# Pairing the projections and re-accounting the filler work in a fused attention and convolution kernel

## The chip, the core and the metric

The kernel runs on one core of a Trainium2 chip, in float32. The metric is device time in microseconds (us), the median of several executions. TensorE does the matrix products, VectorE (DVE) and ScalarE (ACT) the elementwise work, SyncE (SP) issues the loads and stores. GpSimd does almost nothing here. [...]

## The reference

Four layers run one after the other on 16 images of 384 channels and 16 x 16 pixels, seen as 2 clips of 8 frames.

```python
# layer 0: attention over the 2048 pixels of a clip, 12 heads of 32 channels, no value projection
qk = (xt @ qk_w.T).reshape(B, N, 2, nh, HEAD_DIM)
attn = softmax(einsum('bhnd,bhmd->bhnm', q * scale, k), axis=-1)
attn = alpha * eye + beta * attn - gamma * Cm          # Cm is 1/N everywhere
out = einsum('bhnm,bhmd->bhnd', attn, v)               # v is the input itself
# layer 1: 7x7 depthwise convolution, layer norm, 384 -> 1536 -> 384 with gelu and a response norm, residual
# layer 2: Sobel edges, 768 -> 384, layer norm, gelu, residual
# layer 3: 1x1, 3x3 depthwise, 1x1, linear attention, projection, layer norm, MLP 384 -> 1536 -> 384
```

## The kernel before, in words

The pixels of a clip are 4 blocks of 512 (`BLK`). A *unit* of attention is one clip and one group of 128 channels (4 heads); there are 6 units, so 24 blocks of queries. For each block the kernel goes through 16 key tiles of 128. One such round is a *step*, so attention has 384 steps.

In a step `scores` (line 435) makes the scores of four heads in two tiles `st` of two PSUM banks each (from `bank2`, line 385, a pool of three tiles), and ScalarE writes their exponentials to two tiles `e`. `weighted` (line 453) works one step behind: four products of exponentials and values into `av`, then VectorE's adds, which sum the exponentials over groups of four steps in the tiles `s` (steps 1, 2 and 3 of each group have a pair of adds). The sums go through TensorE into the denominators `dn` in four quarter-wide pieces, one per step, the first two steps after the group's last add; the last group of a block goes in one wide piece. `due` is a table from step number to such later work. `finish` (line 508) reads `dn` to `r` on ScalarE; four reciprocals, the scaling of `va` and the write to `l` follow on VectorE, one per step. In `scale` (line 519) ScalarE also passes over `r` to a tile `junk` for the sum that a safety check needs.

Queries and keys of a unit are projected by `qk` (line 397): three products of 128 channels into one bank, then a copy, on ScalarE for a query and on VectorE for a key. The first block of keys and queries and the other keys are needed when a unit starts, the other queries during it. They are called at the steps that `SLOTS` names: steps 0, 4 and 8 of a unit's first block, 0 and 4 of the second and third, 0 of the fourth.

`fill` (line 1444) is called at the end of each step with the projection's time in `added`. It places other work between: the taps of layer 1's 7 x 7 convolution (`convolutions`, line 829; one ScalarE operation and 48 VectorE operations `y<-l` per channel group), and every fourth step one operation of `lead`, layer 1's first block. A single running credit, `room`, says how many taps may be placed. When attention is over, a planner (`Plan.all`, line 180) orders all the remaining work by estimated start times, with the ranks in `RANK` and the tolerance `SLACK`. TensorE, ScalarE and VectorE then run exactly the order in which the program issued the work.

After attention the names are: `ph_l` and `po_l` for layer 1's two wide products, `su` and `sv` for the sums behind a layer norm, `pf` for layer 2, `l3a`, `l3b`, `l3c` for layer 3, whose last part is the MLP with `ph_l3c` and `po_l3c`.

Of the kernel before, what the change touches and what calls it, by code (L numbers as in the profile page):

```python
# [11 lines left out]
ALU = mybir.AluOpType  # L12
# [5 lines left out]
NC = C // P  # L18
# [10 lines left out]
NBLK = N // BLK  # L29
NIP = NBLK  # L30
NQC = N // P
SLOTS = ((0, 4, 8), (0, 4), (0, 4), (0,))
FIRST = NQC + 10

TURNS = (
# [6 lines left out]
    (0, ((1, 1), (1, 2), (1, 3),)),  # L42
    (1, ((0, 3), (1, 0), (1, 3), (1, 2), (1, 1),)),
)
AFTER = ('hid', 0, 2, 1)

RANK = {
    "mid": ((-4.2, 20.2, -65.9, 40.3), (11.6, 63.7, 50.6, 36.1)),
    "l1": ((-28.5, 90.6, 6.7, 64.2), (55.1, 56.5, 16.9, 27.6)),
    "l3c": ((32.8, 24.4, 106.0, 83.3), (3.4, 80.2, 74.5, 60.5)),  # L50
    "conv": 93.3,
}
SLACK = 0.142
JUNK = 2
ADDS = ((4, 4, 4, 4), (4, 4, 4, 4))
XB, YB, SB = 12, 2, 22
TB = BLK // P
RB = 2 * HW
# [132 lines left out]
            self.step(min((s for s in starts if s[0] <= first), key=lambda s: (s[1], s[0]))[2])  # L191


class Task:


    def __init__(self, name, rank, ops):
        self.name, self.rank, self.ops = name, rank, ops
        self.head = next(ops, None)

    def advance(self):
        self.head = next(self.ops, None)


def channel_means(dve, pool, X, cols, b):
# [162 lines left out]
def attention(tc, X, xt, L0, block, small, col, cols, ones, load_qk, banks, fill, bound):  # L368
# [6 lines left out]
    with ExitStack() as actx:  # L375
# [9 lines left out]
        def bank2(name):  # L385
            return pst.tile([P, 2, BLK], F32, tag="st", name=name)
# [4 lines left out]
        def projections(b, g):  # L391


            made = {w: [None] * NBLK for w in "qkv"}
            u = b * NC + g

            def qk(j, n):
                w = "qk"[j]
                pp = bank2(f"p{w}_{u}_{n}")
                for c in range(NC):  # L400
                    pe.matmul(
                        pp[:, 0, :],
                        wqk_sb[:, g, j, c, :],
                        X[b][n][:, c, :],
                        start=(c == 0),
                        stop=(c == NC - 1),
                    )
                o = made[w][n] = small(f"{w}_{u}_{n}")
                (act.copy if j == 0 else dve.tensor_copy)(o, pp[:, 0, :])
                return 2.7 - 0.6 * j  # L410

            def values(n):
                o = made["v"][n] = small(f"v_{u}_{n}")
                nc.sync.dma_start(o, xt[b, g, n])

            def key(n):
                values(n)
                return qk(1, n)

            step = lambda f, *a: lambda: f(*a)  # L420
            early = [step(key, 0), step(qk, 0, 0)] + [step(key, n) for n in range(1, NBLK)]
            late = [step(qk, 0, n) for n in range(1, NBLK)]
            return made, early, late

# [3 lines left out]
        def unit(u, made, gm):  # L428

            b, g = units[u]  # L430
            q, keys, v = made["q"], made["k"], made["v"]
            adds = ADDS[b]
            acc, sums = {}, {}

            def scores(n, t):
# [17 lines left out]
            def weighted(n, t, es):  # L453
                if t == 0:
                    acc["av"] = pacc.tile([P, BLK], F32, tag="av", name=f"av_{u}_{n}")
                for h in range(4):
                    pe.matmul(
                        acc["av"][HD * h : HD * (h + 1), :],
                        v[t // TB][:, (t % TB) * P + HD * h : (t % TB) * P + HD * (h + 1)],
                        es[h // 2][:, h % 2, :],  # L460
                        start=(t == 0),
                        stop=(t == NQC - 1),
                    )
                at = t % adds[n]
# [12 lines left out]
                if at == adds[n] - 1:  # L477
                    parts = 1 if t == NQC - 1 else adds[n]
                    for i in range(parts):
                        due.setdefault(k + 2 + i, []).append(  # L480
                            lambda i=i, summed=dict(sums): weights(
                                n, t, summed, ts(i, BLK // parts)
                            )
                        )
# [23 lines left out]
            def finish(n, va, xg):  # L508

                if g == 0:  # L510
                    L0[b][n] = block(f"l0_{b}_{n}")
                k = u * NBLK + n
                r = op.tile([P, BLK], F32, tag="r", name=f"r_{u}_{n}")
                act.activation(r, acc["dn"], AF.Identity, accum_out=bound[:, 0, k : k + 1])

                def invert(i):
                    dve.reciprocal(r[:, ts(i, P)], r[:, ts(i, P)])

                def scale():
                    junk = op.tile([P, BLK], F32, tag="junk", name=f"junk_{u}_{n}", bufs=1)  # L520
                    act.activation(junk, r, AF.Identity, accum_out=bound[:, 1, k : k + 1])
                    dve.tensor_tensor(va, va, r, ALU.mult)

                def put():
                    dve.scalar_tensor_tensor(
                        L0[b][n][:, g, :], va, col("beta", g), xg, ALU.mult, ALU.add
                    )

                todo = [*(lambda i=i: invert(i) for i in range(TB)), scale, put]
                for i, f in enumerate(todo):  # L530
                    due.setdefault((k + 1) * NQC + 2 + i, []).append(f)

            return scores, weighted
# [2 lines left out]
        for b, (_, steps) in enumerate(means):  # L536
            for i, s in enumerate(steps):
                due[b * NC * NBLK * NQC - 36 * b + 3 * i] = [s]
        made, early, late_steps = projections(*units[0])
        for s in early:  # L540
            s()
        before = None
        for u, (b, g) in enumerate(units):
            steps = late_steps
            scores, weighted = unit(u, made, means[b][0][:, g : g + 1])
            if u + 1 < len(units):
                made, early, late_steps = projections(*units[u + 1])
                steps = steps + early
            for n in range(NBLK):
                for t in range(NQC):  # L550
                    es = scores(n, t)
                    added = 0.0
                    if before:
                        before()
                    before = lambda f=weighted, a=(n, t, es): f(*a)
                    if t in SLOTS[n]:
                        added = steps.pop(0)() if steps else 0.0
                    fill((u * NBLK + n) * NQC + t, added)
            assert not steps
        before()  # L560
# [7 lines left out]
def conv_seq_kernel(  # L568
# [869 lines left out]
    if fast:  # L1438
        open_pool("s", SB)
        open_pool("tiny", 2)  # L1440

        room = 0.0

        def fill(t, added=0.0):
            nonlocal room
            if t < 0:
                while plan.step(bias):
                    pass
                return


            if t % NQC == 9 and t > NQC:
                u, i = divmod(t // NQC - 1, NBLK)
                plan.mark(("l0", u // NC, i, u % NC))
            room = min(3.0, room + 2.25 + added - 2.28 * (t % 4 != 1) - 0.8 * (2 < t % NQC < 9))
            if NC * NBLK * NQC - 36 < t <= NC * NBLK * NQC - 21 and t % 3 == 0:
                room -= 1.7
            if ("y", 0, 0, NC - 1) in plan.made and t % 4 == 1 and plan.holds(lead, "wa"):
                room -= lead.head.length if lead.head.engine == "DVE" else 0.0
                plan.step(lead)  # L1460
            while t >= FIRST and room > 0 and ("y", 0, YB - 1, NC - 1) not in plan.made:
                if not plan.step(conv):
                    break
                room -= 0.57

        attention(
            tc, X, xt, L0, block, small, col, cols, ones, first_loads, banks, fill, bound
# [132 lines left out]
```

## Time and profile before

| | us |
|---|---|
| median of three executions | 2695.55 |
| lowest and highest | 2694.98, 2695.66 |
| the profiled execution: its time | 2696.76 |
| its span, first to last instruction | 2695.0 |
| attention, first score to first hidden product of layer 1 | 22.6 to 1061.4 |
| busy: ScalarE, whole span | 1560.4 |
| adds of exponentials on VectorE (384 and 192) | 444.8 and 225.6 |
| taps of the 7 x 7 convolution on VectorE (1152) | 658.9 |

The profile gives one execution. Busy time of TensorE comes from modelled ends of pipelined products, so that a product which waits for the next can look busy. Each product of float32 appears as two records. In the lists, `out<-in` names the tiles, the number after the bar is the sum of busy time and the mean of one, and the last part is the idle time of the engine just before and what ended it. All arithmetic instructions carry the line of one helper (L96), so tiles are the names to go by.

### The profile page before, as it was taken

The numbers are of one execution on the slowest core, as the hardware profiler recorded it, in microseconds if no ns is written. First come the engines' busy times: TensorE is split into PE (matmuls) and PEld (weight loads), VectorE is DVE, ScalarE is ACT, GpSimd is POOL, SyncE is SP. The second block draws the span as 40 slices with busy tenths as digits, with TensorE's granted clock in tenths as the row PEclk, the third lists the DMA queues.
The fourth block names the chain that finished last, engine by engine and source line by source line (L and its number), as shares of the span: only waits on it lengthen the run. The fifth ranks groups of instructions, "written<-read, shape, count | busy, mean of one in ns | idle before, by whom it ended". The sixth has DMA issues, their size and how long they took to land. (4 is left out here: it accounts for less than half of the span.)

```text
span 2695.0 us, 33760 instructions
## 1 busy us (share of the span) xinstructions
PE 2656.3 (99%) x13477; PEld 1069.1 (40%) x13477; DVE 1996.9 (74%) x2586; ACT 1560.4 (58%) x2282; POOL 7.4 (0%) x54
## 2 busy tenths in 40 slices
PE   9999999999999999999999999999999999999999
PEld 3333333333332323445444444444454444454443
DVE  5899999999999989799999669999904535313120
ACT  5787787778877787565645372533665633125221
POOL 0000000000000000000000000000000000000000
PEclk9999999999999999999999999999999999999999
DMA  3000000000000002100111112121000110000000
GB/s 149 1 17 1 5 13 1 13 5 2 16 1 1 13 1 95 35 0 1 36 36 36 39 46 68 59 71 47 16 8 0 35 36 0 12 1 13 12 4 21
DMA packets 34421, 65.17 MB, mean 24 GB/s; under 512 B 1872, under 2 KB 17360, under 8 KB 34256
## 3 DMA queue, kind: packets, MB, share of 16 engines
q1 hardware_dynamic: 34112, 62.79, 7.1%
q8 instruction: 107, 1.75, 0.3%
q14 instruction: 58, 0.48, 0.1%
q10 hardware_dynamic: 144, 0.15, 0.0%
HBM read 56.64 MB, written 6.29 MB: 23 GB/s over the span
## 5 line engine op out<-in xcount | busy, mean ns | idle before, releaser
L96 ACT ACTIVATE e<-st 128x1024 f32<-128x1024 f32 x768 | 743.5, 1022 | 175.5 <-PE st L96 169.7
L96 DVE SCALAR_TENSOR_TENSOR y<-l,vec,y 128x420 f32<-128x420 f32 (+8 forms) x1152 | 658.9, 632 | 18.8 <-ACT y L96 13.4
L96 PE MATMUL st<-q,k 32*128 32x512 f32 x3072 | 464.5, 643 | 8.6 <-DVE k L96 3.3
L96 DVE TENSOR_TENSOR s<-s,e 128x1024 f32<-128x1024 f32 x384 | 444.8, 1209 | 2.8 <-ACT e L96 2.8
L96 PE MATMUL av<-e,v 128*32 128x512 f32 x3072 | 411.9, 607 | 0.7 <-ACT va L96 0.7
L96 PE MATMUL po_l<-hid_l,wb 128*128 128x512 f32 x576 | 258.2, 602 | 7.3 <-ACT hid_l L96 7.2
L96 PE MATMUL ph_l<-y,wa 128*128 128x512 f32 x576 | 258.6, 594 | 1.0 <-ACT y L96 1.0
L96 PE MATMUL ph_l3c<-d_l3c,wa 128*128 128x512 f32 x576 | 257.2, 593 | 0.0
L96 PE MATMUL po_l3c<-hid_l3c,wb 128*128 128x512 f32 x576 | 254.1, 593 | 0.0
L96 DVE TENSOR_TENSOR s<-e,e 128x1024 f32<-128x1024 f32 x192 | 225.6, 1216 | 33.0 <-PE dn L96 19.3
L96 ACT ACTIVATE hid_l3c<-ph_l3c,vec 128x512 f32<-128x512 f32 x96 | 65.8, 686 | 248.0 <-PE ph_l3c L96 247.8
L96 PEld LDWEIGHTS st<-q,k 32*128 32x128 f32 x3072 | 137.1, 183 | 170.3 <-issue 99.9
L96 PEld LDWEIGHTS av<-e,v 128*32 128x32 f32 x3072 | 60.6, 108 | 294.0 <-issue 286.1
L96 PEld LDWEIGHTS po_l<-hid_l,wb 128*128 128x128 f32 x576 | 110.4, 193 | 145.9 <-issue 131.5
L96 PEld LDWEIGHTS ph_l3c<-d_l3c,wa 128*128 128x128 f32 x576 | 108.9, 190 | 136.5 <-issue 129.8
L96 PEld LDWEIGHTS ph_l<-y,wa 128*128 128x128 f32 x576 | 108.3, 190 | 137.2 <-issue 126.2
L96 PEld LDWEIGHTS po_l3c<-hid_l3c,wb 128*128 128x128 f32 x576 | 108.7, 190 | 133.2 <-issue 129.6
L96 PEld LDWEIGHTS dn<-s,ones 128*32 128x32 f32 x2496 | 81.8, 111 | 187.4 <-issue 174.5
L96 DVE SCALAR_TENSOR_TENSOR o_l3c<-po_l3c,vec,l 128x512 f32<-128x512 f32 x24 | 17.6, 742 | 170.7 <-PE po_l3c L96 170.0
L96 PE MATMUL dn<-s,ones 128*32 128x128 f32 (+1 forms) x2496 | 142.4, 299 | 0.0
L96 ACT ACT_TABLE_LOAD x103 | 132.1, 1283 | 7.5 <-PE ph_l L96 5.4
L96 ACT ACTIVATE hid_l<-ph_l,vec 128x512 f32<-128x512 f32 x96 | 65.6, 683 | 119.4 <-PE ph_l L96 118.8
(155 smaller groups left out, 2480.5 us busy)
## 6 DMA issues: line engine op xcount, KB each, us to landing
wa<-in_w_dram SPq DMA_DIRECT2D x12, 768.0 KB, 4.5
wb<-in_w_dram SPq DMA_DIRECT2D x12, 768.0 KB, 4.6
wa<-in_mlp_w_dram SPq DMA_DIRECT2D x12, 768.0 KB, 4.5
wb<-in_mlp_w_dram SPq DMA_DIRECT2D x12, 768.0 KB, 4.5
x<-in_x_dram SPq DMA_DIRECT2D x8, 768.0 KB, 10.7
v<-in_xt_dram SPq DMA_DIRECT2D x24, 256.0 KB, 2.7
out_dram<-o_l3c SPq DMA_DIRECT2D x24, 256.0 KB, 2.0
qkv<-in_qkv_wT_dram SPq DMA_DIRECT2D x3, 576.0 KB, 11.1
```

What stands on the lines that cost most here:

```text
L96: self.last = self.tc.keep_in_program_order(make(*args, **kw))
```

## The change

The projections are made in pairs: one tile of two banks takes two of them, and there is one pair per block of queries, at step 5. The keys and queries of the opening are paired too. The credit of `fill` is replaced by an account: `pace` gives for each step the time of TensorE and of VectorE, what VectorE is behind is carried to the next step as `lag`, and taps are placed while at least 0.4 us is free. A tap that must wait for the one before costs 0.12 more in the account. The first operation of a chunk, on ScalarE, ends a step's placing. The pass over `r` for the check stands in a function of its own and is due four steps later. `ADDS` has another form with the same values. The ranks, the tolerance and the point after which the second clip's convolution may begin (`AFTER`) have other values.

```diff
-SLOTS = ((0, 4, 8), (0, 4), (0, 4), (0,))
+SLOT = 5
-AFTER = ('hid', 0, 2, 1)
+AFTER = ('x4', 0, 1)
 RANK = {
...
-SLACK = 0.142
+SLACK = 0.122
...
+def pace(t):
+    n, i = divmod(t - 1, NQC)
+    adds = ADDS[n]
+    stride = adds // 4
+    pe, dve = 2.066, 2.275 if t and i % adds else 0.0
+    at = i - adds - 1
+    if at >= 0 and at % adds % stride == 0 and at % adds < 4 * stride and i > adds:
+        pe += 0.22
+    elif i == 1 and n > 0:
+        pe += 0.87
+    else:
+        pe += 0.09
+    if n > 0:
+        dve += {2: 0.88, 3: 0.88, 4: 0.88, 5: 0.88, 6: 0.6, 7: 0.66}.get(i, 0.0)
+    return pe, dve
...
-            def qk(j, n):
+            def qk(j, n, pp):
                 w = "qk"[j]
-                pp = bank2(f"p{w}_{u}_{n}")
                 for c in range(NC):
                     pe.matmul(
-                        pp[:, 0, :],
+                        pp,
...
-                (act.copy if j == 0 else dve.tensor_copy)(o, pp[:, 0, :])
+                (act.copy if j == 0 else dve.tensor_copy)(o, pp)
                 return 2.7 - 0.6 * j
...
                 def scale():
+                    dve.tensor_tensor(va, va, r, ALU.mult)
+
+                def check():
                     junk = op.tile([P, BLK], F32, tag="junk", name=f"junk_{u}_{n}", bufs=1)
                     act.activation(junk, r, AF.Identity, accum_out=bound[:, 1, k : k + 1])
-                    dve.tensor_tensor(va, va, r, ALU.mult)
...
-                for i, f in enumerate(todo):
+                for i, f in [*enumerate(todo), (8, check)]:
                     due.setdefault((k + 1) * NQC + 2 + i, []).append(f)
...
+        def project(name, steps):
+            pp = bank2(name)
+            return sum(f(pp[:, i, :]) for i, f in enumerate(steps))
+
         made, early, late_steps = projections(*units[0])
-        for s in early:
-            s()
+        for i in range(0, len(early), 2):
+            project(f"p_{i}", early[i : i + 2])
...
-                    if t in SLOTS[n]:
-                        added = steps.pop(0)() if steps else 0.0
+                    if t == SLOT and steps:
+                        added = project(f"p_{u}_{n}", steps[:2])
+                        del steps[:2]
                     fill((u * NBLK + n) * NQC + t, added)
...
-            room = min(3.0, room + 2.25 + added - 2.28 * (t % 4 != 1) - 0.8 * (2 < t % NQC < 9))
-            if NC * NBLK * NQC - 36 < t <= NC * NBLK * NQC - 21 and t % 3 == 0:
-                room -= 1.7
+            length, work = pace(t)
+            free = length + added - work - lag
+            if NC * NBLK * NQC - 36 < t <= NC * NBLK * NQC - 21 and t % 3 == 1:
+                free -= 1.7
             if ("y", 0, 0, NC - 1) in plan.made and t % 4 == 1 and plan.holds(lead, "wa"):
-                room -= lead.head.length if lead.head.engine == "DVE" else 0.0
-                plan.step(lead)
-            while t >= FIRST and room > 0 and ("y", 0, YB - 1, NC - 1) not in plan.made:
+                if plan.step(lead) and lead.at.engine == "DVE":
+                    free -= lead.at.length
+            ops = []
+            while t >= FIRST and ("y", 0, YB - 1, NC - 1) not in plan.made:
+                op = conv.head
+                if op.engine == "DVE":
+                    if free < 0.4:
+                        break
+                    free -= op.length + 0.12 * (op.after[0] in ops[-1:])
                 if not plan.step(conv):
                     break
-                room -= 0.57
+                ops.append(op)
+                if op.engine == "ACT" and conv.head.engine == "DVE":
+                    break
+            lag = max(0.0, -free)
```

More of the change, by code (lines that the diff above doesn't have):

```diff
@@ L44 @@
 )
-AFTER = ('hid', 0, 2, 1)
+AFTER = ('x4', 0, 1)
 RANK = {
[L48 to L51, printed above, removed]
+    "mid": ((-16.9, 20.2, -65.9, 50.2), (11.6, 60.8, 50.6, 36.1)),
+    "l1": ((-41.0, 15.6, 6.7, 54.8), (53.9, 56.5, 16.9, 46.3)),
+    "l3c": ((37.9, 24.4, 106.0, 83.2), (3.4, 41.2, 70.0, 60.5)),
+    "conv": 97.9,
 }
-SLACK = 0.142
+SLACK = 0.122
 JUNK = 2
-ADDS = ((4, 4, 4, 4), (4, 4, 4, 4))
+ADDS = (4,) * 24
 XB, YB, SB = 12, 2, 22
@@ L191, in all @@
             self.step(min((s for s in starts if s[0] <= first), key=lambda s: (s[1], s[0]))[2])
+def pace(t):
[13 more added lines that the diff above has]
+    return pe, dve
 class Task:
     def __init__(self, name, rank, ops):
-        self.name, self.rank, self.ops = name, rank, ops
+        self.name, self.rank, self.ops, self.at = name, rank, ops, None
         self.head = next(ops, None)
     def advance(self):
-        self.head = next(self.ops, None)
+        self.at, self.head = self.head, next(self.ops, None)
 def channel_means(dve, pool, X, cols, b):
@@ L414, in values, with key @@
                 nc.sync.dma_start(o, xt[b, g, n])
-            def key(n):
+            def key(n, pp):
                 values(n)
-                return qk(1, n)
-            step = lambda f, *a: lambda: f(*a)
+                return qk(1, n, pp)
+            step = lambda f, *a: lambda pp: f(*a, pp)
             early = [step(key, 0), step(qk, 0, 0)] + [step(key, n) for n in range(1, NBLK)]
@@ L431, in unit @@
             q, keys, v = made["q"], made["k"], made["v"]
-            adds = ADDS[b]
+            adds = ADDS[u * NBLK : (u + 1) * NBLK]
             acc, sums = {}, {}
@@ L477, in weighted @@
                 if at == adds[n] - 1:
-                    parts = 1 if t == NQC - 1 else adds[n]
+                    parts = 1 if t == NQC - 1 else 4
                     for i in range(parts):
-                        due.setdefault(k + 2 + i, []).append(
+                        due.setdefault(k + 2 + i * adds[n] // 4, []).append(
                             lambda i=i, summed=dict(sums): weights(
@@ L1440, in conv_seq_kernel @@
         open_pool("tiny", 2)
-        room = 0.0
+        lag = 0.0
         def fill(t, added=0.0):
-            nonlocal room
+            nonlocal lag
             if t < 0:
```

## The prediction

> **What bounds the kernel now.** I read the page first, then the windows by stage, then the groups by line, then the timeline. The page's row of TensorE and the windows of attention, handover, and the two later stretches:
>
> ```profile
> PE 2656.3 (99%) x13477; PEld 1069.1 (40%) x13477; DVE 1996.9 (74%) x2586; ACT 1560.4 (58%) x2282; POOL 7.4 (0%) x54
> ...
> 28.00:1061.40 1033.40, 1024.16 (x8881) 323.61 (x8873) 960.46 (x1031) 819.85 (x943) 0.00 (x0) 1.00 0.02 6
> 1061.40:1125.00 63.60, 54.88 (x135) 24.55 (x134) 47.15 (x73) 47.60 (x109) 0.00 (x0) 0.92 0.38 135
> 1125.00:1620.00 495.00, 486.99 (x1425) 223.79 (x1424) 437.70 (x674) 269.05 (x482) 2.55 (x18) 0.99 0.09 28
> 1620.00:2690.00 1070.00, 1068.59 (x2988) 488.19 (x2986) 545.56 (x787) 417.33 (x740) 4.19 (x30) 1.00 0.08 24
> ```
>
> The columns are TensorE, weight loads, VectorE, ScalarE, GpSimd, granted clock, DMA share, GB/s. TensorE is the bound everywhere, and from 1125 us on it is nearly seamless (about 9 us idle in 1565). So the change can win only in attention and the handover. In attention VectorE is busy 960 of 1033 us, so a second engine runs close behind.
>
> "99%" hides stalls, because a modelled matmul can stretch. I took the distance from each step's first score matmul to the next. A bare step is 2.066 us, one with the quarter sums (dn) 2.286, the one with the wide dn 2.94, and a projection adds 2.77. The floor of attention is then 384 x 2.066 + 24 x (12 x 0.22 + 0.87) + 43 x 2.77 = 996.6 us. Observed, from the first score at 22.6 to the first hidden matmul at 1061.4, it is 1038.8. So 42 us are stall. Where they come from is seen in one block:
>
> ```profile
> 436.90 1.14 PE L96 MATMUL st<-q,k 32*128 32x512 f32 x8
> 437.97 1.06 PE L96 MATMUL av<-e,v 128*32 128x512 f32 x8
> 438.03 0.95 DVE L96 RECIPROCAL r<-r 128x128 f32<-128x128 f32 x1
> 438.85 0.40 PE L96 MATMUL dn<-s,ones 128*32 128x128 f32 x8
> 438.89 2.29 DVE L96 TENSOR_TENSOR s<-s,e 128x1024 f32<-128x1024 f32 x2
> 439.01 0.63 ACT L96 ACTIVATE junk<-r 128x512 f32<-128x512 f32 x1 [1.28 <-DVE r L96]
> 439.18 1.13 PE L96 MATMUL st<-q,k 32*128 32x512 f32 x4
> 439.55 0.19 ACT L96 ACTIVATION_READ_ACCUMULATOR junk<-r 128x1 f32 x1
> 439.64 3.75 ACT L96 ACTIVATE e<-st 128x1024 f32<-128x1024 f32 x4
> 440.70 1.13 PE L96 MATMUL st<-q,k 32*128 32x512 f32 x4 [0.39 <-ACT e L96]
> ```
>
> The check sum (junk) stands in ScalarE's queue ahead of the next exponentials and waits for VectorE's last reciprocal. The exponentials come late, the score banks stay full, and the second half of the scores starts 1.5 us after the first. Steps 9 of all blocks hold 13 of the 42 us; most of the rest lies in steps 4 to 8.
>
> The copies out of a projection, which the change moves:
>
> ```profile
> L96 DVE COPY k<-pk 128x512 f32<-128x512 f32 x24 | 16.2, 676 | 34.0 <-PE pk L96 34.0
> L96 ACT COPY q<-pq 128x512 f32<-128x512 f32 x24 | 14.1, 586 | 47.0 <-PE pq L96 47.0
> ```
>
> Both engines already stand still for TensorE there. In the timeline a copy starts 0.11 us after the next score matmul (pq from 602.93, scores 605.70, q 605.81).
>
> [...] The halves of a pair are two banks[...]; no run here shows whether one is placed. In the built order of the changed kernel one is: the first matmul of each second half lists a wait on ScalarE (on VectorE where the first half is a key). The slot's earlier reader is a ScalarE exponential, so at the key pairs nothing but the first half's copy explains VectorE. [...] the trace agrees with six windows (or runs) of 3.41 us at half clock after stalls, the one around 1116 us three windows long.
>
> **The change, part by part.** The built lists hold the same instructions before and after. Only order differs; after 1.15 ms only some VectorE neighbours swap and, at the very end, hidden matmuls of the last block alternate with output matmuls of the one before. TensorE is seamless there and the inputs (d_l3c) are ready at 2590 for 2596: nothing gained or lost.
>
> *Check sum later.* It now stands at step 11, when the reciprocals are long done. What remains of the 42 us: the score-exponential loop at step 4 (0.17 x 24 = 4), layer 1's two early sums (2 us of matmul and about 4 of table loads on ScalarE), the drain at the end (3). So 29 of 42 go: **-29** (22 to 33).
>
> *Pairs.* Two halves of six passes at 0.427 us are 2.56 each, plus 0.21 for changing tile form. Between them TensorE waits: the last pass ends, the copy starts (0.11 after the point where scores would start), lasts 0.59, and is seen about 0.05 later; against an unbroken stream that is 1.0, with the slower first pass 1.1 us. A pair takes 2.56 + 1.1 + 2.56 + 0.21 = 6.43 against 2 x 2.77 = 5.54: 0.89 x 21 = **+18.7** (10 to 26; below 0.7 the copy alone forbids). Behind the wait stand scores, hence everything. In the five key-key pairs VectorE must first work off its queue: summing its rows from one dn to the next it arrives about 0.9 late, **+4** (0 to 8). The three opening pairs have two such waits: **+2**.
>
> *Taps by the account.* In 13 of the blocks a key is the last half of the pair, so VectorE's copy stands until the projection ends, 2 to 5 us idle, and the 4 to 8 taps that the account grants for the projection's time stand behind the copy. From the start of the next step S: copy 0.11 + 0.61, taps n x 0.66 (start to start within one chunk; 0.55 where two chunks alternate), then adds of steps 5 to 7, a reciprocal and va: 8.3 us from the first to the last end in the block above (435.76 to 444.06). The sums are ready at S + 9.0 + taps. TensorE wants them at S + 4 x 2.286 + 2.05 = S + 11.2, 11.1 with the signal. So 2.1 us of taps are free. The list has 6, 5, 6, 6, 5, 6, 5, 8, 6, 7, 7, 6 taps there, and 4 plus two channel means (1.66 each) in the thirteenth: stalls of 1.7, 1.2, 1.45, 1.9, 1.2, 1.45, 1.2, 2.3, 1.2, 1.9, 1.8, 1.2 and 3.7, together **+22** (6 to 30). In before such sums ended up to 1.1 after the step began, about 1 us inside the limit, so it was not binding. Blocks whose pair is two queries escape.
>
> *Handover.* 266 taps stand before the last add, against 279; layer 1's first block starts later (its sum moved by 24 steps), so its last scaling falls behind the final check sum:
>
> ```profile
> 1061.39 10.57 PE L96 MATMUL ph_l<-y,wa 128*128 128x512 f32 x24
> 1074.18 1.12 PE L96 MATMUL su_l<-s_l,ones 128*128 128x512 f32 x2 [2.22 <-DVE s_l L96]
> ...
> 1065.71 0.63 ACT L96 ACTIVATE junk<-r 128x512 f32<-128x512 f32 x1 [3.52 <-DVE r L96]
> ```
>
> From the end T of attention, the first hidden column stops at its third chunk until junk (T + 4.9) and a scaling of 0.8 are done: 4 us. VectorE then does 4.9 of finish, 18 taps (10.4), weight means (5.8), the weight scaling (1.5), 4 taps and two adds (3.6): su at T + 27, TensorE there at T + 24. Then sv at T + 34, the next block's scaled input at T + 46, po at T + 53.1, where it was 1108.9, T + 47.5: **+5.6** (2 to 9). TensorE's weights arrive earlier (ca lands near T + 18), so no DMA decides.
>
> *Sum.* -29 + 18.7 + 4 + 2 + 22 + 5.6 = +23 on the profiled span of 2695.0, whose execution took 2696.8; the median of the three is 2695.55. Carried to the median: 2719. Attention would end near 1079.
>
> **Rivals.** *The pair wait alone* (chance 0.17): the sums come in time, since VectorE had 73 us idle in attention and the late-sum figure rests on a chain of six durations. For it: dn waited for s only 8 us before. Against: the taps stand behind the copy. 2719 - 22 = 2697.
> *Faster* (0.10), one mechanism: the second half of a pair doesn't really wait, its place being the listed wait on ScalarE. If this were the old exponential, long over, the pair saves 0.21 x 21 = 4.4, TensorE gives VectorE time for the taps and the sums come within the limit; -29 - 4.4 + 5.6 gives 2668. It decides once a first copy lands before its second half's first pass. Against: VectorE is named at the key pairs.
> *Half clock* (0.15): 34 new stalls of 1 to 4 us, and each window of 3.41 us at half costs 1.7. Before, stalls of 2 to 5 us were followed by one, one of 2.2 at 1072 was not. Ten more give +17: 2736.
>
> **How the numbers follow.** The forecast (0.58) is 2719, by itself 2706 to 2732. About 0.2% (5.4 us) is what a measurement of this kernel tells from no change. The pair wait alone splits into 0.03 faster, 0.09 same, 0.05 slower; so faster 0.13, same 0.09, slower 0.78. A range of 2692 to 2738 leaves out the faster case and the ends, about 0.18.
>
> **What would show it.** Right: some 21 idle times of about 1 us of TensorE before p, ended by copies of q (16) or k (5); dn waiting for s by some 20 us in all; junk's idle time (9 us before) near nothing; ph_l stopped some 4 us by y. Wrong: pairs of 5.3 us, attention ending before 1050, or new losses after 1150 us, which would mean that the later order matters more than its few swaps suggest.

## The result and the profile after

The changed kernel takes 2737.65 us (median of 4 runs, 2735.56 to 2737.73) against 2695.27 for the kernel before (4 runs): ratio 1.0156, interval 1.0138 to 1.0174. It is slower by 42 us where 23 were forecast. The profiled execution has a span of 2735.8 us where before had 2695.0.

First the page's rows of TensorE and VectorE, then the same four stages as windows (columns as before: TensorE, weight loads, VectorE, ScalarE, GpSimd, granted clock, DMA share, GB/s). Attention now ends at 1095.3 us.

```profile
PE 2665.1 (97%) x13477; PEld 1070.3 (39%) x13477; DVE 1997.9 (73%) x2586; ACT 1557.4 (57%) x2282; POOL 7.4 (0%) x54
...
30.00:1095.30 1065.30, 1031.11 (x8875) 325.13 (x8871) 951.51 (x1018) 814.98 (x941) 0.00 (x0) 1.00 0.02 6
1095.30:1166.00 70.70, 56.81 (x138) 25.18 (x137) 55.50 (x86) 48.90 (x110) 0.00 (x0) 0.95 0.34 121
1166.00:1661.00 495.00, 486.98 (x1422) 223.79 (x1421) 439.27 (x678) 268.86 (x482) 2.55 (x18) 0.99 0.09 28
1661.00:2730.00 1069.00, 1068.42 (x2987) 488.11 (x2986) 544.01 (x785) 417.29 (x740) 4.19 (x30) 1.00 0.07 24
```

TensorE is 97% busy instead of 99, and the missing time lies in the first two windows: in attention it idles for 34 us of 1065 instead of 9. The last two stages are as they were. The end of attention moved by 33.9 us (1061.4 to 1095.3), and what follows it takes 6.9 us more (1633.6 to 1640.5).

The groups of instructions that the prediction named, in the changed kernel:

```profile
L97 PE MATMUL dn<-s,ones 128*32 128x128 f32 (+1 forms) x2496 | 147.2, 298 | 13.5 <-DVE s L97 13.3
L97 PE MATMUL p<-x,wqk_sb 128*128 128x512 f32 x288 | 138.5, 619 | 17.5 <-ACT q L97 10.8 <-DVE k L97 5.5 <-DMA x<-in_x_dram 1.2
L97 DVE COPY k<-p 128x512 f32<-128x512 f32 x24 | 16.6, 692 | 89.5 <-PE p L97 72.1 <-issue 17.4
L97 ACT ACTIVATE junk<-r 128x512 f32<-128x512 f32 x24 | 15.2, 632 | 3.5 <-DVE r L97 3.5
```

TensorE stood 16.3 us before p for the copies, 23 times (nothing before), and 13.3 before dn for the sums (nothing before; about as much again shows as waits of dn's weight loads). VectorE's idle time before the key copies rose from 34.0 to 89.5 us. The check sum waits 3.5 us, all of it in the last block, instead of 9.0.

One block with a query and a key in its pair, from the timeline (start, length, engine, in brackets the idle time before and what ended it; here and below, lines between those shown are left out):

```profile
667.62 2.84 PE L97 MATMUL p<-x,wqk_sb 128*128 128x512 f32 x6
670.50 0.59 ACT L97 COPY q<-p 128x512 f32<-128x512 f32 x1 [1.77 <-PE p L97]
671.14 2.84 PE L97 MATMUL p<-x,wqk_sb 128*128 128x512 f32 x6 [0.68 <-ACT q L97]
673.91 1.14 PE L97 MATMUL st<-q,k 32*128 32x512 f32 x8
674.07 0.69 DVE L97 COPY k<-p 128x512 f32<-128x512 f32 x1 [5.85 <-issue]
674.68 4.16 DVE L97 SCALAR_TENSOR_TENSOR y<-l,vec,y 128x390 f32<-128x390 f32 x8
678.75 2.36 DVE L97 TENSOR_TENSOR s<-e,e 128x1024 f32<-128x1024 f32 x2
...
684.69 2.36 DVE L97 TENSOR_TENSOR s<-s,e 128x1024 f32<-128x1024 f32 x2
685.97 0.41 PE L97 MATMUL dn<-s,ones 128*32 128x128 f32 x4 [0.40 <-DVE s L97]
687.10 0.41 PE L97 MATMUL dn<-s,ones 128*32 128x128 f32 x4 [0.72 <-DVE s L97]
```

The second half starts when the first half's copy is done (671.14 after 670.50 + 0.59). VectorE stands for 5.85 us, copies the key, and only then runs eight taps and the three pairs of adds of a group; dn, due at 685.57 when the products av of 684.50 are done, waits twice for them.

What the prediction had not seen is the turn of a block, two steps long:

```profile
612.26 0.60 ACT L97 ACTIVATE va<-av 128x512 f32<-128x512 f32 x1
612.74 0.82 ACT L97 ACTIVATE xg<-x,gm,vec 128x512 f32<-128x512 f32 x1
612.91 1.06 PE L97 MATMUL av<-e,v 128*32 128x512 f32 x8 [0.23 <-ACT va L97]
613.44 3.81 ACT L97 ACTIVATE e<-st 128x1024 f32<-128x1024 f32 x4
614.13 1.52 PE L97 MATMUL st<-q,k 32*128 32x512 f32 x8
```

The first av of the new block waits for the copy va of the old one (one accumulator), and va and xg put 1.4 us into ScalarE's queue, so that four exponentials run without a gap and the next scores are stretched from 1.14 to 1.52. In the kernel before, a projection stood in step 0 of every block but the last three, va and xg ran beside its 2.77 us, and neither was seen: at 594.48 av starts without a wait. In its last blocks, without a projection there, the same two losses stand (from 1023.59 on):

```profile
591.60 1.88 PE L96 MATMUL pk<-x,wqk_sb 128*128 128x512 f32 x4
591.82 0.82 ACT L96 ACTIVATE xg<-x,gm,vec 128x512 f32<-128x512 f32 x1
594.48 1.06 PE L96 MATMUL av<-e,v 128*32 128x512 f32 x8
...
1023.59 0.82 ACT L96 ACTIVATE xg<-x,gm,vec 128x512 f32<-128x512 f32 x1
1023.77 1.06 PE L96 MATMUL av<-e,v 128*32 128x512 f32 x8 [0.23 <-ACT va L96]
1024.98 1.52 PE L96 MATMUL st<-q,k 32*128 32x512 f32 x8
```

The same sum as in the prediction, for every run: the distance between the first score matmuls of neighbouring steps, less the floor of the step, added over the 24 blocks. T is the end of attention, "rest" the span after it. All in us, each row from one trace; the median is that of all runs of the kernel.

| kernel | steps 0-3 | 4 | 5 | 6-8 | 9-11 | 12-15 | sum | T | rest | median |
|---|---|---|---|---|---|---|---|---|---|---|
| before | 2.7 | 4.9 | 4.8 | 12.3 | 14.1 | 3.8 | 42.8 | 1061.4 | 1633.6 | 2695.3 |
| changed | 16.0 | 4.2 | 16.5 | 0.4 | 26.7 | 10.8 | 74.5 | 1095.3 | 1640.5 | 2737.65 |
| e1 before, check sum later | 3.5 | 4.9 | 4.7 | 12.3 | 8.2 | 5.7 | 39.3 | 1057.5 | 1633.4 | 2692.7 |
| e7 before, pairs | 16.9 | 4.7 | 17.2 | 0.2 | 56.4 | 18.3 | 113.7 | 1133.7 | 1632.3 | 2768.5 |
| e9 before, pairs, check sum later | 16.9 | 4.7 | 17.7 | 0.2 | 24.6 | 20.3 | 84.5 | 1105.2 | 1631.7 | 2738.7 |
| e8 changed, single projections | 5.1 | 5.3 | 2.5 | 5.0 | 1.4 | 7.5 | 26.8 | 1045.8 | 1632.8 | 2682.4 |
| e2 changed, matmuls first | 16.0 | 4.2 | -3.8 | 1.2 | 33.1 | 10.6 | 61.1 | 1079.7 | 1640.2 | 2720.5 |
| e3 changed, taps first | 16.5 | 4.2 | 21.1 | 0.4 | 2.5 | 11.6 | 56.3 | 1077.0 | 1640.9 | 2718.4 |
| e4 changed, xg later | 7.5 | 4.2 | 16.5 | 0.9 | 25.4 | 10.6 | 65.0 | 1085.8 | 1641.4 | 2729.5 |
| e5 = e2 + e3 + e4 | 8.2 | 4.2 | -3.8 | 0.9 | 2.7 | 11.4 | 23.6 | 1041.5 | 1639.5 | 2683.5 |
| e6 = e2 + e3, pair in step 0 | -2.6 | 4.1 | 0.0 | 5.5 | 4.6 | 10.6 | 22.3 | 1041.1 | 1633.7 | 2676.9 |
| e10 = e6, check sum in step 0 | -1.4 | 4.1 | 0.0 | 5.5 | 4.6 | 8.7 | 21.7 | 1040.0 | 1633.8 | 2675.55 |
| e11 changed, scaling ahead of check sum | 16.9 | 4.2 | 16.5 | 0.4 | 27.0 | 11.0 | 76.0 | 1096.4 | 1641.4 | 2737.2 |
| e12 changed, old ranks | 16.0 | 4.2 | 16.5 | 0.4 | 25.4 | 10.6 | 73.1 | 1093.3 | 1640.8 | 2735.7 |

A pair with no wait falls 0.19 below the floor: the floor counts for each projection what its two ends take above the 0.429 us from pass to pass (0.427 in the prediction), and a pair has them once. In the kernel before the second pass starts 0.533 us after the first and the next score 0.522 after the last pass, together 0.197 more (0.21 in the prediction, which puts it down to the tile form; behind a copy of the changed kernel's pairs, with no change of form, a first pass took 0.533 too). The floor of the very last step leaves out its three narrow pieces of dn, so each sum stands 0.7 above what the prediction's floor gives (42.2 for before). In e7 and e9 the last step alone loses 15.2 us: there the wait for layer 1's first input stands ahead of T, and the rest is shorter for it.

### The profile page after: what moved, and what is told of

Read it like the earlier page. It is cut to its first block, busy times and chain, and to the rows that moved or that the text cites. A ratio compares the mean times of both kernels' runs of the same rounds, so it can differ in the third digit from the quotient of the medians.

```text
span 2735.8 us, 33756 instructions
## 1 busy us (share of the span) xinstructions
PE 2665.1 (97%) x13477; PEld 1070.3 (39%) x13477; DVE 1997.9 (73%) x2586; ACT 1557.4 (57%) x2282; POOL 7.4 (0%) x54
## 5 line engine op out<-in xcount | busy, mean ns | idle before, releaser
L97 PE MATMUL dn<-s,ones 128*32 128x128 f32 (+1 forms) x2496 | 147.2, 298 | 13.5 <-DVE s L97 13.3
L97 PE MATMUL p<-x,wqk_sb 128*128 128x512 f32 x288 | 138.5, 619 | 17.5 <-ACT q L97 10.8
```

The costliest lines, as they stand in the source:

```text
L97: self.last = self.tc.keep_in_program_order(make(*args, **kw))
```

## The experiments

**Where the three losses of attention come from (e2, e3, e4).** Each takes one suspected wait out of the changed kernel.

e2 issues all passes of a pair ahead of its copies:

```diff
-                o = made[w][n] = small(f"{w}_{u}_{n}")
-                (act.copy if j == 0 else dve.tensor_copy)(o, pp)
-                return 2.7 - 0.6 * j
+
+                def copy():
+                    o = made[w][n] = small(f"{w}_{u}_{n}")
+                    (act.copy if j == 0 else dve.tensor_copy)(o, pp)
+                    return 2.7 - 0.6 * j
+
+                return copy
...
-            return sum(f(pp[:, i, :]) for i, f in enumerate(steps))
+            copies = [f(pp[:, i, :]) for i, f in enumerate(steps)]
+            return sum(c() for c in copies)
```

> The changed kernel with all twelve passes of a pair issued ahead of its two copies. Theory (the second half of a pair waits for the copy of the first because both lie in one tile): the loss at step 5, 0.75 to 0.86 us in each of 20 pairs, and about 2 us in the opening go, time about 2719. Rival 1 (the pair's extra time is the first pass and the clock, not the wait): no change, 2737. Rival 2 (the time comes back as later sums, because both copies now stand ahead of the taps): sums for dn later by up to 0.6 us in 13 blocks, 2727.

Measured 2720.5 us, ratio to before 1.0092 (1.0075 to 1.0108). TensorE no longer waits before p, but more before dn:

```profile
L97 PE MATMUL dn<-s,ones 128*32 128x128 f32 (+1 forms) x2496 | 146.9, 298 | 15.8 <-DVE s L97 15.8
L97 PE MATMUL p<-x,wqk_sb 128*128 128x512 f32 x288 | 132.8, 612 | 1.2 <-DMA x<-in_x_dram 1.2
L97 DVE COPY k<-p 128x512 f32<-128x512 f32 x24 | 16.0, 689 | 82.3 <-ACT q L97 49.6 <-PE p L97 32.7
```

The theory holds for step 5 of the 21 pairs (16.5 to -3.8: 20.3 us), the opening gives 2.2, and rival 2 is true beside it: steps 9 to 11 rose from 26.7 to 33.1. The key's copy now waits for the query's copy (49.6 us of idle time ended by ACT q), so the taps and sums start 0.6 us later.

e3 issues the same taps ahead of the pair (`f.cost` is the time that `qk` returned):

```diff
...
-                        added = project(f"p_{u}_{n}", steps[:2])
-                        del steps[:2]
+                        added = sum(f.cost for f in steps[:2])
                     fill((u * NBLK + n) * NQC + t, added)
+                    if t == SLOT and steps:
+                        project(f"p_{u}_{n}", steps[:2])
+                        del steps[:2]
```

> The changed kernel with the same taps in the same step, issued ahead of the projections and so ahead of the copy of the key. Theory (taps stand behind the key's copy, and the sums behind the taps, so dn waits at step 10): the 24 us lost in steps 9 and 10 fall below 4, VectorE's idle time before the key copies falls from 90 us by some 45, time about 2716. Rival 1 (VectorE has too much work in these steps wherever the taps stand): under 8 us gained, 2730 or more. Rival 2 (the copies, now behind the taps and scalings, hold the pair's banks and so the scores of step 6): a new loss at steps 5 to 7 of about 1 us each, 2730.

Measured 2718.4, ratio 1.0083 (1.0066 to 1.01). Steps 9 to 11 fell from 26.7 to 2.5 us and VectorE's idle time before the key copies from 89.5 to 57.1:

```profile
L97 PE MATMUL dn<-s,ones 128*32 128x128 f32 (+1 forms) x2496 | 141.6, 298 | 0.0
L97 PE MATMUL p<-x,wqk_sb 128*128 128x512 f32 x288 | 138.4, 618 | 22.1 <-ACT q L97 10.8 <-DVE k L97 10.1 <-DMA x<-in_x_dram 1.2
L97 DVE COPY k<-p 128x512 f32<-128x512 f32 x24 | 16.5, 689 | 57.1 <-PE p L97 53.3 <-issue 3.8
```

So the sums were late because of the taps' place, not of VectorE's total work. 4.6 us came back at the five pairs of two keys, where the first copy now stands behind the taps and the second half behind that copy (k 5.5 to 10.1).

e4 issues xg five steps later, ahead of the pair:

```diff
-                    act.activation(
-                        xg, X[b][n][:, g, :], AF.Identity, scale=col("alpha", g), bias=gm
-                    )
+                    due.setdefault(k + 5, []).append(
+                        lambda: act.activation(
+                            xg, X[b][n][:, g, :], AF.Identity, scale=col("alpha", g), bias=gm
+                        )
+                    )
```

> The changed kernel with the activation xg (0.82 us on ScalarE), which stands behind the copy of av at the turn of a block, issued five steps later, ahead of the pair. Theory (before, a projection in step 0 of every block gave ScalarE the time for va and xg; the change took this cover away, and steps 1 and 2 now lose 0.30 and 0.37 us in 22 blocks): step 1 loses nothing, step 2 less than 0.37, 7 to 14 us gained, 2724 to 2731. Rival 1 (the loss is in dn and the copy of av, xg has no part in it): no change, 2737. Rival 2 (xg ahead of the pair delays the copy of the query there): step 5 loses 0.8 more in 16 blocks, 2735 to 2745.

Measured 2729.5, ratio 1.0126 (1.0109 to 1.0143): 8.1 us gained. The loss at step 2 went (0.37 to 0), but step 1 kept its 0.30 where none was expected. The same turn in e4:

```profile
606.69 1.94 ACT L97 ACTIVATE e<-st 128x1024 f32<-128x1024 f32 x2
606.83 1.07 PE L97 MATMUL av<-e,v 128*32 128x512 f32 x8 [0.23 <-ACT va L97]
```

The turn is thus two losses: ScalarE's backlog, which xg made, and the accumulator, which av must have back from va.

**Do they add up, and is it the cover (e5, e6).** e5 is the three edits together. e6 is e2 and e3 with one size changed:

```diff
-SLOT = 5
+SLOT = 0
```

> The changed kernel with the three edits together: matmuls of a pair ahead of its copies, taps ahead of the pair, xg five steps later. Theory (the losses are independent: pair 0.94 us in 20 pairs and 2 in the opening, late sums 24, xg 0.37 in 23 blocks): attention ends near 1040 us, time near 2681. Rival (one wait behind another: what is taken from one comes back in the next, as late sums did with the matmuls first): 2695 or more.

> The changed kernel with matmuls first and taps first, and the pair in step 0 of a block instead of step 5; xg stays where it was. Theory (a projection gives ScalarE time to catch up, and so covers what follows it): steps 1 and 2, 0.67 us in 22 blocks, lose nothing where a pair stands in step 0, and step 6 loses 0.23 again in some 20 blocks, as before; attention ends near 1042, time near 2683. Rival (the sums of steps 1 to 3, now behind more taps and four reciprocals, come late for dn at step 6): 1 us or more at step 6 in most blocks, 2700 or more.

e5: 2683.5, ratio 0.9958 (0.9942 to 0.9975). e6: 2676.9, ratio 0.9929 (0.9913 to 0.9946). The three losses add up: each column of e5 is as low as in the run that took that loss alone, or nearly. The times gain more than they did singly (17.2, 19.2 and 8.1 us make 44.5, together 54.1), because the side effects go too: once e3 stands beside it, e2's later sums no longer matter (9-11 at 2.7), and with e2 the copies that e3 delayed hold nothing up. In e6 steps 1 to 3 lose 2.5 us instead of 17.1, and steps 6 to 8 lose 5.5 instead of 0.4: the cover moved with the pair, and is worth more at the turn. (The two edits with the pair left in step 5 were not run; e5 has the xg edit besides, and e6 is 6.6 us below it.) Its turn:

```profile
619.31 5.42 PE L97 MATMUL p<-x,wqk_sb 128*128 128x512 f32 x12
619.46 4.69 DVE L97 SCALAR_TENSOR_TENSOR y<-l,vec,y 128x390 f32<-128x390 f32 x9
620.02 0.60 ACT L97 ACTIVATE va<-av 128x512 f32<-128x512 f32 x1
620.50 0.82 ACT L97 ACTIVATE xg<-x,gm,vec 128x512 f32<-128x512 f32 x1
624.66 1.14 PE L97 MATMUL st<-q,k 32*128 32x512 f32 x8
624.76 0.59 ACT L97 COPY q<-p 128x512 f32<-128x512 f32 x1 [3.44 <-PE p L97]
625.38 0.69 DVE L97 COPY k<-p 128x512 f32<-128x512 f32 x1 [1.24 <-ACT q L97]
```

Taps, va and xg all run beside the twelve passes, and nothing of TensorE's is behind them. The rival of e6 (late sums at step 6) did not come: VectorE has done nine of its taps before the pair ends.

**Which part of the change brings the loss (e1, e7, e8, e9).** e1 and e9 take only the later check sum, into the kernel before and into e7:

```diff
                 def scale():
-                    junk = op.tile([P, BLK], F32, tag="junk", name=f"junk_{u}_{n}", bufs=1)
-                    act.activation(junk, r, AF.Identity, accum_out=bound[:, 1, k : k + 1])
                     dve.tensor_tensor(va, va, r, ALU.mult)
+
+                def check():
+                    junk = op.tile([P, BLK], F32, tag="junk", name=f"junk_{u}_{n}", bufs=1)
+                    act.activation(junk, r, AF.Identity, accum_out=bound[:, 1, k : k + 1])
...
-                for i, f in enumerate(todo):
+                for i, f in [*enumerate(todo), (8, check)]:
```

e7 takes only the pairs:

```diff
-SLOTS = ((0, 4, 8), (0, 4), (0, 4), (0,))
+SLOT = 5
...
-                    if t in SLOTS[n]:
-                        added = steps.pop(0)() if steps else 0.0
+                    if t == SLOT and steps:
+                        added = project(f"p_{u}_{n}", steps[:2])
+                        del steps[:2]
```

e8 is the changed kernel with this last edit undone, one projection for each tile of two banks. (The check sum of e1 comes four steps behind the scaling, not six as its expectation says.)

> The kernel before with one part of the change alone: the check sum (junk) is issued at step 10 of the block, six steps after the scaling, instead of ahead of it. Theory (the check sum held ScalarE's queue and with it the exponentials): steps 4 to 9, which lose 35.4 us above the floor in the kernel before, fall to about 6, attention is 29 us shorter, time about 2666. Rival 1 (only the visible wait of step 9 goes): 13 us, 2682. Rival 2 (the sums or VectorE are as late as the check sum was and take its place): under 5 us, 2690 or more.

> The kernel before with the pairs of the change alone (one pair in step 5, both halves in one tile, copy after each half); its check sum and its way of placing taps are kept. Theory (the pairs bring nearly all of the loss, the late sums too, because taps are placed behind the key's copy whatever counts them): step 5 loses 0.75 to 0.86, steps 1 and 2 0.67, steps 9 and 10 together about 1 in most blocks; time 2725 to 2740. Rival (the late sums come from the new account, which grants more taps): steps 9 and 10 lose little beyond the check sum's 0.4, time about 2715.

> The changed kernel with single projections in the steps of the kernel before (0, 4 and 8; 0 and 4; 0 and 4; 0) instead of pairs; account, ranks and check sum as changed. Theory (the pairs bring nearly all of the loss): attention ends near 1052 as in the kernel before with only the check sum moved, the handover keeps its 5.7 us, time about 2698, at most 2705. Rival (the account makes sums late at single projections too, now at step 6): 2712 or more.

> The kernel before with the pairs and the later check sum, its own way of placing taps kept: run e7 plus the edit of run e1. Theory (the check sum costs what VectorE is late: with pairs, reciprocals and sums stand behind the taps, so ScalarE waits for the reciprocal in most blocks; moved, only the lateness of the sums is left): steps 9 and 10, 56 us in e7, fall to 25 or 30, time about 2740. Rival (moving the check sum is worth the same 3 us with and without pairs): 2765.

e1: 2692.7 (20 runs), ratio 0.9989 (0.9982 to 0.9996). This is rival 2's number: 3 us and not 29. Step 9 alone fell from 13.4 to 5.5, what is left being one block's 5.5; but steps 10 and 13 rose by 1.9 and 2.4, because sums were as late as the check sum in a few blocks, and because its 0.83 us (0.63 and 0.20 for the read-out) push ScalarE back in step 13 (0.11 us a block) as they did in step 9. Steps 4 to 8 lose 22 us as before.

e7: 2768.5, ratio 1.0272 (1.0255 to 1.0289), beyond the 2740 expected. e9: 2738.7, ratio 1.016 (1.0145 to 1.0176), as expected. The check sum's group in e7 and in e9:

```profile
L96 ACT ACTIVATE junk<-r 128x512 f32<-128x512 f32 x24 | 15.1, 631 | 36.9 <-DVE r L96 36.9
```

```profile
L96 ACT ACTIVATE junk<-r 128x512 f32<-128x512 f32 x24 | 15.2, 633 | 3.5 <-DVE r L96 3.5
```

In the old place it waits 36.9 us once the pairs are there, against 9.0 without them, since the reciprocals then stand behind the taps. So the same edit is worth 3 us with single projections and 30 with pairs. But not all of the 30 is waiting. In e7's trace TensorE runs twelve windows of 3.41 us at half clock in attention, ahead of the last block (mean granted clock of the execution 0.987, 0.994 in e9); they begin in step 9 of ten blocks, each within 2 us of an idle time of 1.1 to 1.8 us of TensorE that the late exponentials end. One of the ten, where the products av behind the wait take 1.87 us instead of 1.07:

```profile
468.83 0.63 ACT L96 ACTIVATE junk<-r 128x512 f32<-128x512 f32 x1 [2.39 <-DVE r L96]
470.51 1.13 PE L96 MATMUL st<-q,k 32*128 32x512 f32 x4 [1.49 <-ACT e L96]
471.57 1.87 PE L96 MATMUL av<-e,v 128*32 128x512 f32 x8
```

e9 has no such window there. TensorE was busy through nearly all of the twelve, so half of their time, some 20 us, is an estimate of what they cost. The expectation of e7 had no term for this, and the time lies beyond it. Late sums are there under the old account too (e9: 24.6 in steps 9 to 11, changed 26.7), so the account does not cause them; the pair's place between VectorE and its taps does.

e8: 2682.4, ratio 0.9954 (0.9937 to 0.997), 16 us below what was expected. Beside e1 the rest of the change (account, ranks, `AFTER`) takes another 10.3 us off (steps 9 to 11 from 8.2 to 1.4, steps 6 to 8 from 12.3 to 5.0; mostly in blocks 10 and 19 to 21, where the means and layer 1's early sums lie). In just these blocks e1 has three windows at half clock, by the same estimate 5.1 us, and e8 has none (mean granted clock 0.994 and 0.998). The handover did not keep its 5.7 us: e8's rest is 1632.8. The pairs by themselves, from e8 to the changed kernel, cost 55.3 us.

**The handover (e11) and the ranks (e12).** e11 issues layer 1's last scaling in the last step of attention, ahead of the last check sum; e12 puts back the ranks and the slack of the kernel before.

```diff
-            if ("y", 0, 0, NC - 1) in plan.made and t % 4 == 1 and plan.holds(lead, "wa"):
+            if ("y", 0, 0, NC - 1) in plan.made and (t % 4 == 1 or t >= NC * NBLK * NQC * NB - 1) and plan.holds(lead, "wa"):
```

> The changed kernel with layer 1's last scaling of y_0 issued in the last step of attention, ahead of the last check sum instead of behind it. Theory A, the prediction's (VectorE's 22 taps decide when su and all behind it run; the stop of ph_l by 3.8 us only fills time that TensorE would wait for su anyway): ph_l no longer stops, su starts still 28.9 us after attention's end, its wait grows from 2.9 to about 6.7, time 2737. Theory B (the place of the scaling costs what it shows): su comes when TensorE comes, 3 to 4 us gained, 2734.

> The changed kernel with the ranks and the slack of the kernel before. Theory (the later order is worth nothing, as TensorE is nearly seamless from 1150 us on; only the last hidden columns of the last block stand elsewhere on it): within 1.5 us of 2737.6. Rival (the new ranks cost or gain in the last 1090 us): a difference of 3 us or more.

In the changed kernel the stop and then su:

```profile
1099.61 0.63 ACT L97 ACTIVATE junk<-r 128x512 f32<-128x512 f32 x1 [3.52 <-DVE r L97]
1100.24 0.80 ACT L97 ACTIVATE y<-y,vec 128x512 f32<-128x512 f32 x1
1101.09 2.26 PE L97 MATMUL ph_l<-y,wa 128*128 128x512 f32 x3 [3.81 <-ACT y L97]
...
1124.22 1.10 PE L97 MATMUL su_l<-s_l,ones 128*128 128x512 f32 x2 [2.85 <-DVE s_l L97]
```

In e11:

```profile
1096.43 20.87 PE L97 MATMUL ph_l<-y,wa 128*128 128x512 f32 x48
1119.07 2.82 PE L97 MATMUL ph_l<-y,wa 128*128 128x512 f32 x6
1125.37 2.05 PE L97 MATMUL su_l<-s_l,ones 128*128 128x512 f32 x2 [3.49 <-DVE s_l L97]
```

The stop is gone, and su still starts 28.9 us after attention's end (1125.37 - 1096.43; changed 1124.22 - 1095.30 = 28.9). That su waits 3.49 and not 6.7 is because 54 hidden matmuls now stand ahead of it, where 42 did. So VectorE's taps set su, as theory A has it. But the stop was not free. Those hidden matmuls are done early, po starts at T + 52.5 instead of T + 54.7, and from T + 58 to T + 136 TensorE's work lies 3.8 us nearer to T than in the changed kernel, which is theory B's gain. The profiled execution loses it again near T + 283: there e11 has another order, with nothing between pg_l and po_l, and TensorE waits 2.50 us for hid_l and then runs one window at half clock; the changed kernel has neither (mean granted clock 0.993, 0.996 in the changed kernel). Time 2737.2, ratio 1.0147 (1.0133 to 1.0161), its five runs spread over 10 us, so the time alone tells nothing of 3 us.

e12: 2735.7, ratio 1.015 (1.0136 to 1.0164), 1.9 us below the changed kernel where at most 1.5 were expected. Its rest is 1640.8 against 1640.5; the difference lies in attention, 2 us (T 1093.3), of which 0.5 is the start and 1.3 one window of 3.41 us at half clock (block 10, step 11, from 507.89) that the changed kernel's trace has and this one has not. In what follows attention the ranks make no difference that shows.

**A better kernel (e10).** e6 with the check sum in step 0, ahead of the pair, `(8, check)` becoming `(13, check)`:

> Run e6 with the check sum at step 15 of the block's wait (issued in step 0 ahead of the pair) instead of step 10. Theory (the check sum still costs 0.11 us of scores at step 13 in 20 blocks, because ScalarE has little to spare in a bare step, and a pair hides it): 2.2 us less than e6, near 2674.5. Rival (ScalarE catches up by itself, the 0.11 comes back elsewhere): no change against e6, 2676.9.

Measured 2675.55, ratio to before 0.9924 (0.9911 to 0.9938), 1.3 us below e6, within the spread of both. Steps 12 to 15 fell by 1.9 us as expected, and 1.2 came back at step 1 of blocks 22 and 23, which have no pair to hide it. The tie between e10 and e6 leaves the rival standing. Both e6 and e10 beat both kernels; from the changed one e10 is 62 us away.

## Why the prediction was right in direction and short by half

Slower was right, and the measured +42 lies beyond the single case's 2706 to 2732, and only 0.4 us inside the wide range. The terms that were forecast came to +20.7 against +23.3; the miss is two losses for which there was no term, +13.3 and +7.0. That the forecast terms agree so well is in part luck, as the first one shows. Term by term, in attention and after it:

- *Check sum later, -29*: the step that failed as argued. It took everything that the floor did not explain, less a residual, as the check sum's; e1 shows 3.5 us without the pairs (42.8 to 39.3). The losses of steps 4 to 9 did shrink by 30.8, from 35.4 to 4.6 outside the pair and the sums. From run to run, 8.0 of this came with the later check sum (before to e1; it gave part back in steps 10 and 13), 14.6 with the rest of the change at single projections (e1 to e8; up to 5.1 of it the three windows at half clock), and 8.2 with the pair in step 5, after which steps 6 to 8 lose nothing (5.0 in e8, 0.4 in the changed kernel). And some 5 us was not saved but moved to steps 12 to 15, see below. The size came out by luck; that the check sum was what held these losses in the kernel before was wrong.
- *Pairs, +18.7 and +4*: measured 16.5, and 20.3 against a pair without the wait. Copies of q ended 16 idle times of 0.68 us and copies of k seven of 0.78 (five in pairs, two in the opening). From start to start that is 1.27 us to the next pass behind a copy of q and 0.53 from this one to its follower, where an unbroken stream has 0.43 twice: 0.94, about the 1 us named. VectorE was not 0.9 late at key pairs but 0.1 (0.86 against 0.75). *Opening, +2*: 2.1.
- *Sums behind the taps, +22*: 26.7 in steps 9 to 11, and e3 takes away 24.2 of it by the taps' place alone. The limit worked out from the durations of a block (2.1 us of taps free) was good: in twelve of the thirteen blocks the loss at steps 9 and 10 is within 0.4 us of the stall forecast for that block's number of taps (eight taps: 2.3 forecast, 2.1 measured). In the thirteenth, with the means, it was 2.3 where 3.7 were forecast.
- *The term left out*: what the moved projections had covered. The prediction priced the pair where it went and not the hole where it came from: steps 0 to 3 rose from 2.7 to 16.0, **+13.3**. The trace of before showed it: the last blocks, without a projection in step 0, already lost 0.30 and 0.37 there.
- *Steps 12 to 15, nothing predicted*: +7.0. The check sum's new place accounts for 1.9 (0.11 in 17 blocks). 5.0 come from layer 1's early sums: su stands in step 13 of block 20 and sv in step 9 of block 22, and up to step 15 scores wait for ScalarE behind them (behind sv its two table loads of 1.28 us each, at 1047.13 and 1049.13; the prediction has about 4 us for them). In before su and sv stood in blocks 19 and 21, in steps 5 and 1, and lost their time within steps 1 to 9.
- *Handover, +5.6*: +5.7 up to the middle of the later stages, and 1.3 from three more passes at half clock around 545 us after attention's end (6.83 us at half clock from 1641.12, where the kernel before has 3.41 from 1602.88). The stop of 3.8 us was seen (4 forecast), su at T + 28.9 (27), po at T + 54.7 (53.1). VectorE does set su, but e11 shows that the stop itself is worth 3.8 us, where the prediction let VectorE decide all that follows.
- *Half clock* was no cost in the changed kernel: attention has one such window (from 507.89) where before had three (from 479.89, 875.84 and 961.17), each 3.41 us long, and the mean granted clock rose from 0.994 to 0.996. The long run at half clock that the prediction puts around 1116 us stands at 1104.5 to 1114.8. The rival *faster* fell with the 21 waits; *the pair wait alone* fell with dn.

Added up: -30.8 + 16.5 + 2.1 + 26.7 - 0.7 + 13.3 + 7.0 + 6.9 = 41.0, where the spans differ by 40.8; 0.7 is what steps 10 and 11 lost before.

What stays open: which of account, ranks, `AFTER` and order of first taps makes the 10 us between e1 and e8 (e12 put back ranks and slack in the changed kernel alone), and whether the second half of a pair could run beside the copy of the first if they were two tiles; neither was tried.

## What to carry to other kernels

When work moves from one place to another, price the place that it leaves: list what the other engines did beside it, and look for a block that never had it. A loss above a floor belongs to nobody until a run takes the suspect away; here one edit was worth 3 us in one surrounding and 30 in another. Where an engine's copy must wait for a long piece of work on another, put its independent work ahead of the copy in its queue, not behind it, unless somebody waits for the copy itself: e3 gained 24.2 us in the sums so, and lost 4.6 at the five pairs whose second half waited for that copy.

## What the runs showed of the hardware and was not expected

Two engines that only read the same tile were put one behind the other: VectorE's key copy started at 625.38, when ScalarE's query copy (624.76 + 0.59) was done. In both e6 and e2 the trace has the key copy wait for the semaphore that the query copy raises; in e2 ten key copies were released so, about 0.6 us later than the passes would have let them. The two halves are parts of one tile; that the wait stands for this reason is the author's estimate, as no run gave them two.

ScalarE's spare time in a bare step is so small (two exponentials take 1.94 of 2.07 us) that the check sum's 0.63 us with its read-out costs TensorE 0.11 us in step 13, and nothing where a pair follows it (e6 to e10, steps 12 to 15: 10.6 to 8.7). At the turn of the two blocks without a pair the same activation cost 0.60 in e10, since va and xg already stand there.

Idle times of 1.1 to 1.8 us were followed by half clock in one place and not in another. In attention of e7, ahead of the last block, ten of the twelve idle times of TensorE over 1 us had a window at half clock within 2 us (mean granted clock 0.987); in e3, none of the five of 1.5 to 1.8 us did (0.995). Nor did the sum of idle time tell it: TensorE of the changed kernel idles for 34 us in attention, with no piece over 0.95 us, and has one such window there. What decides between them no run shows.
